# Layer 1's dense products cut into four of 32 outputs each, placed in the column groups of the PE array

## The chip, the core and the metric

The kernel runs on one core of a Trainium2 chip. A core has a tensor engine (PE, a 128 x 128 array that multiplies a stationary operand, loaded by its own weight-load instruction, with a moving operand, and writes to the PSUM memory), a vector engine (DVE), a scalar engine (ACT), a general engine (POOL) and queues for transfers. The metric is the device time of one execution in microseconds (us).

## What is computed

Two attention layers over x of shape (1, 128, 256, 256), that is 128 rows of 256 positions with 256 channels. Layer 0 is an attention with bias and gate. The change touches layer 1 alone:

```python
x = x + layer1(group_norm(x))            # layer1 for each of the 128 rows:
qkv = x2 @ w_in.T + b_in                 # 256 -> 3 * 256
q, k, v = split(qkv, 3)                  # four heads of 64
scores = q @ k.T / sqrt(64)              # only where |i - j| <= 16
out = softmax(scores) @ v
y = out @ w_out.T + b_out
```

All operands are float32.

## The kernel before

Layer 1 goes through the 128 rows in 64 pairs. The group norm's scale is folded into w_in once, its mean is taken off when a row is turned. `P` is 128, `C` 256, `I` 256, `KC` (chunks of channels) 2, `NB` (blocks of positions in a row) 2, `N2` 512 (positions of a pair), `H1` four heads, `DH` 32. `mm1` gives one of two PSUM banks of 512 columns. In each call of `matmul(out, stationary, moving)` the stationary operand's columns become the partitions of the output.

The parts of `Pair1` that the change touches:

```python
def turn(self, k):                       # channels onto partitions
    ...
    ps = mm1("ps_x1")
    for t in range(2 * NB):
        nc.tensor.transpose(ps[:, t * P : (t + 1) * P], self.xt[:, t, k * P : (k + 1) * P], ident)
    nc.scalar.activation(self.xgT[:, k, :], ps, AF.Identity, bias=nM1[:, k : k + 1])
    ...
def project(self, which, m):             # q and k, transposed
    ...
    for k in range(KC):
        nc.tensor.matmul(
            ps, w_in[:, k, n * C + m * P : n * C + (m + 1) * P], self.xgT[:, k, :],
            start=(k == 0), stop=(k == KC - 1),
        )
    nc.scalar.activation(...)            # ps to SBUF, with the bias
def values(self, r):
    ...
    for b in range(NB):
        t = r * NB + b
        for k in range(KC):
            nc.tensor.matmul(
                ps[:, b * C : (b + 1) * C], self.xgT[:, k, t * P : (t + 1) * P], w_in[:, k, 2 * C : 3 * C],
                start=(k == 0), stop=(k == KC - 1),
            )
    nc.scalar.copy(...)
def out_row(self, r):
    ...
    for b in range(NB):
        for k in range(KC):
            nc.tensor.matmul(
                ps[:, b * C : (b + 1) * C], self.oT[r][:, k, b * P : (b + 1) * P], w_out[:, k, :],
                start=(k == 0), stop=(k == KC - 1),
            )
    nc.vector.tensor_tensor(...)         # add the residual, to the output tile
```

Scores and apply use parts of the array already: scores 64 rows by 64 columns (a head's 64 channels, half of the 128 keys of a block), apply 64 rows by 32 columns. The schedule of one turn of the loop, written by hand:

```python
now.scores(0); was.apply(1); was.out_row(0); was.combine(1)
nxt.project("qT", 0); nxt.project("kT", 0); nxt.project("qT", 1)
nn.turn(0)

now.scores(1); now.apply(0); now.combine(0)
nxt.project("kT", 1); nxt.values(0); nxt.values(1)
was.out_row(1)
nn.turn(1)
```

Layer 0 has one product of the form that the change brings to layer 1, four heads side by side with 32 outputs each, which the prediction refers to:

```python
for b in range(NB):
    for q in range(HQ):                  # HQ = 4, D0 = 32
        h = c * HQ + q
        nc.tensor.matmul(
            ov[q * D0 : (q + 1) * D0, :], self.v[:, r, b, h * D0 : (h + 1) * D0],
            es[q // 2][:, q % 2, b, :], start=(b == 0), stop=(b == NB - 1),
        )
for q in range(HQ):
    nc.tensor.matmul(su[q * D0 : (q + 1) * D0, :], ...)   # sums of the weights, the same way
```

Of the kernel before, what the change touches and what calls it, by code (L numbers as in the profile page):

```python
# [16 lines left out]
P = 128  # L17
# [4 lines left out]
def bcast(ap, axis, n):  # L22

    ap = ap.unsqueeze(axis)
    shape = list(ap.shape)
    shape[axis] = n
    return ap.broadcast_to(shape)
# [746 lines left out]
def fast_kernel(  # L774
# [25 lines left out]
    nc = tc.nc  # L800
    S, I, C = x.shape
# [3 lines left out]
    H1, D1, BAND = 4, 64, 16  # L805
# [3 lines left out]
    KC = C // P  # L809
# [9 lines left out]
    ident = const.tile([P, P], F32, name="ident")  # L819
# [14 lines left out]
    def load_chunks(src, n, name):  # L834
        t = const.tile([P, src.shape[0] // P, n], F32, name=name)
        queued.append((t, src.rearrange("(k p) n -> p k n", p=P)))
        return t
# [71 lines left out]
    def rows(ap, s0, n):  # L909
        return ap[s0 : s0 + n].rearrange("s (b p) c -> p (s b) c", p=P)  # L910
# [17 lines left out]
    w_in = load_chunks(w_inT, 3 * C, "w_in")  # L928

    w_out = const.tile([P, KC, C], F32, name="w_out")  # L930
    for a in range(KC):
        for h in range(H1):
            n = P // H1
# [5 lines left out]
    for h in range(H1):  # L939
        n = P // H1  # L940
# [270 lines left out]
    class Pair:  # L1211
# [48 lines left out]
        def turn(self, pss=None):  # L1260
            self.xgT = la.tile([P, KC, N2], F32, name="xgT", tag="xgT", bufs=2)
            if pss is None:
                ps = ps_s.tile([P, KC, N2], F32, name="ps_x", tag="s")
                pss = [ps[:, k, :] for k in range(KC)]
            for k in range(KC):
                for t in range(NT):
                    nc.tensor.transpose(
                        pss[k][:, t * P : (t + 1) * P], self.xg[:, t, k * P : (k + 1) * P], ident
                    )
            for k in range(KC):  # L1270
                nc.scalar.copy(self.xgT[:, k, :], pss[k])
# [6 lines left out]
        def project(self, which, m):  # L1278
            w, src, b, fn, sc = {
                "gT": (wg, "xgT", bg_c, AF.Tanh, 0.5),  # L1280
                "qT": (wq, "xnT", qb, AF.Identity, 1.0),
                "kT": (wk, "xnT", kb, AF.Identity, 1.0),
            }[which]
            if m == 0:
                pool, bufs = (lb, 1) if which == "gT" else (la, 2)
                setattr(self, which, pool.tile([P, KC, N2], F32, name=which, tag=which, bufs=bufs))
            ps = mm("ps_p")
            for k in range(KC):
                nc.tensor.matmul(  # L1289
                    ps, w[:, k, m * P : (m + 1) * P], getattr(self, src)[:, k, :],  # L1290
                    start=(k == 0), stop=(k == KC - 1),
                )
            nc.scalar.activation(  # L1293
                getattr(self, which)[:, m, :], ps, fn, bias=b[:, m : m + 1], scale=sc
            )

        def values(self, r):
            if r == 0:
                self.v = la.tile([P, 2, NB, C], F32, name="v", tag="v", bufs=2)
            self.ps_v = mm("ps_v")  # L1300
# [4 lines that stand above are left out]
                        self.ps_v[:, b * C : (b + 1) * C], self.xnT[:, k, t * P : (t + 1) * P], wv[:, k, :],  # L1305
                        start=(k == 0), stop=(k == KC - 1),
                    )
# [80 lines left out]
        def out_row(self, r):  # L1388
            nonlocal xo
            s = 2 * self.p + r  # L1390
            if s % GB == 0:
                xo = lb.tile([P, GB * NB, C], F32, name="xo", tag="xo", bufs=2)
            self.ps_y = mm("ps_y")
# [3 lines that stand above are left out]
                        self.ps_y[:, b * C : (b + 1) * C], self.oT[r][:, k, b * P : (b + 1) * P], wo[:, k, :],  # L1397
                        start=(k == 0), stop=(k == KC - 1),
                    )
# [106 lines left out]
    behind, nx, n = None, 0, 0  # L1506
# [41 lines left out]
    with tc.manual_schedule():  # L1548
        old = was = Nobody()
        es = nn3 = None  # L1550
        for p in range(NP):
# [3 lines left out]
            ps = now.scores(0, 0)  # L1555
# [15 lines left out]
            ps = now.scores(0, 1)  # L1571
# [13 lines left out]
            ps = now.scores(1, 0)  # L1585
# [12 lines left out]
            ps = now.scores(1, 1)  # L1598
# [49 lines left out]
    DH = P // H1  # L1648
    LATE = 8
    rsum1 = dram.tile([NP, H1, 2, I], F32, name="rsum1")  # L1650
    with tc.tile_pool(name="l1", bufs=2) as sb, tc.tile_pool(
# [5 lines left out]
        def mm1(name):  # L1657
            return ps_mm.tile([P, 512], F32, name=name, tag="mm")
# [4 lines left out]
        for k in range(KC):  # L1663
            ps = mm1("ps_mr")
# [9 lines left out]
        for n in range(2):  # L1674
            nc.vector.memset(o_eo[n], 0.0)
            nc.vector.memset(su_eo[n], 0.0)

        class Pair1:


# [7 lines left out]
            def turn(self, k):  # L1688
                if k == 0:
                    self.xgT = sb.tile([P, KC, N2], F32, name="xgT1", tag="xgT")  # L1690
                ps = mm1("ps_x1")
                for t in range(2 * NB):
                    nc.tensor.transpose(ps[:, t * P : (t + 1) * P], self.xt[:, t, k * P : (k + 1) * P], ident)  # L1693
                nc.scalar.activation(self.xgT[:, k, :], ps, AF.Identity, bias=nM1[:, k : k + 1])  # L1694
                if k == KC - 1:
                    nc.gpsimd.tensor_tensor(self.xt, self.xt, bcast(bout_r, 1, 2 * NB), ALU.add)  # L1696

            def project(self, which, m):
                n = ("qT", "kT").index(which)
                if m == 0:  # L1700
                    setattr(self, which, sb.tile([P, KC, N2], F32, name=f"{which}1", tag=which))
                ps = mm1("ps_p1")
                for k in range(KC):
                    nc.tensor.matmul(  # L1704
                        ps, w_in[:, k, n * C + m * P : n * C + (m + 1) * P], self.xgT[:, k, :],
                        start=(k == 0), stop=(k == KC - 1),
                    )
                nc.scalar.activation(
                    getattr(self, which)[:, m, :], ps, AF.Identity, bias=bin_c[:, n * KC + m : n * KC + m + 1]
                )  # L1710

            def values(self, r):
                if r == 0:
                    self.v = sb.tile([P, 2, NB, C], F32, name="v1", tag="v")
                ps = mm1("ps_v1")
                for b in range(NB):
                    t = r * NB + b
                    for k in range(KC):
                        nc.tensor.matmul(  # L1719
                            ps[:, b * C : (b + 1) * C], self.xgT[:, k, t * P : (t + 1) * P], w_in[:, k, 2 * C : 3 * C],  # L1720
                            start=(k == 0), stop=(k == KC - 1),
                        )
                nc.scalar.copy(self.v[:, r, :, :].rearrange("p b c -> p (b c)"), ps)

            def scores(self, r):
# [60 lines left out]
            def out_row(self, r):  # L1786
                if r == 0:
                    self.yo = sb.tile([P, 2 * NB, C], F32, name="yo", tag="yo")
                ps = mm1("ps_y1")
                for b in range(NB):  # L1790
                    for k in range(KC):
                        nc.tensor.matmul(  # L1792
                            ps[:, b * C : (b + 1) * C], self.oT[r][:, k, b * P : (b + 1) * P], w_out[:, k, :],
                            start=(k == 0), stop=(k == KC - 1),
                        )
                nc.vector.tensor_tensor(  # L1796
                    self.yo[:, r * NB : (r + 1) * NB, :], ps.rearrange("p (b c) -> p b c", b=NB),
                    self.xt[:, r * NB : (r + 1) * NB, :], ALU.add,
                )
                s0 = 2 * self.p  # L1800
                if self.p == NP - 1:
                    nc.sync.dma_start(rows(out, s0 + r, 1), self.yo[:, r * NB : (r + 1) * NB, :])
                elif r == 1:
                    nc.sync.dma_start(rows(out, s0, 2), self.yo)
# [81 lines left out]
        ps = mm1("ok_ps")  # L1886
# [4 lines left out]
@with_exitstack  # L1891
def mixer_kernel(ctx, tc, *args):

    nc = tc.nc
    keep = ctx.enter_context(tc.tile_pool(name="verdict", bufs=1))
    verdict = keep.tile([1, 1], mybir.dt.int32, name="verdict")
    fast_kernel(tc, *args, verdict)
    again = nc.values_load(verdict[0:1, 0:1], min_val=0, max_val=1)
    with tc.If(again > 0):
        general_kernel(tc, *args)  # L1900
# [53 lines left out]
```

## Time and profile before

| | |
|---|---|
| time, median of 3 runs | 3370.32 us (3369.57 to 3371.17) |
| profiled span | 3366.7 us |
| PE busy | 3221.6 us, 96% of the span |
| weight loads (PEld) busy | 2032.1 us, 60% |
| DVE busy | 2024.1 us, 60% |
| ACT busy | 1463.3 us, 43% |
| POOL busy | 1975.2 us, 59% |
| mean granted PE clock | 0.983 |

Layer 1's first product starts at about 2119 us, and the rest of the span belongs to it. In the profile's names L1693 is the transposes (tile `ps_x`), L1704 the projections (`ps_p`), L1719 the values (`ps_v`), L1792 the output (`ps_y`), L1733 the scores (`ps_sc`), L1761 apply (`ps_o`, and `ps_su` for its sums). A group's row gives line, engine, operation, output and inputs, for a product the rows * columns of the array that it uses, partitions x elements, the count, busy time, mean length of one, and the idle time before it. Products overlap and their ends are modelled, so what a stage costs is read from the start of its first product to the start of the next stage.

### The profile page before, as it was taken

What the parts mean: (1) busy time and instruction counts of PE and PEld (TensorE: products, weight loads), DVE (VectorE), ACT (ScalarE), POOL (GpSimd) and SP (SyncE); (2) the same over time, 40 slices, a digit from 0 to 9 for tenths busy, and PEclk for the clock granted to TensorE, in tenths of its full rate; (3) what the DMA queues carried; (4) which work ended last, traced back from release to release, by engine and by line L of the source; (5) the groups of instructions that cost most, each with busy time, mean ns of one, the idle gap of its engine ahead of it and who ended that gap; (6) DMA issues with size and microseconds to landing.
All of it is one profiled execution on the core that took longest, in us unless ns stands there. A gap on an engine that the chain in (4) does not pass through costs nothing. (4 is left out here: it accounts for less than half of the span.)

```text
span 3366.7 us, 81193 instructions
## 1 busy us (share of the span) xinstructions
PE 3221.6 (96%) x35158; PEld 2032.1 (60%) x35158; DVE 2024.1 (60%) x3218; ACT 1463.3 (43%) x2121; POOL 1975.2 (59%) x1377
## 2 busy tenths in 40 slices
PE   5389999999999999999999998899999999999998
PEld 3245555555555555555555554567767777677676
DVE  7966666666666666666666666366544444443456
ACT  2264444444444444444444443344444444444443
POOL 2378787777777787887777874333333333333332
PEclk8699999999999999999999999999999999999999
DMA  9951212221222222122212221211211211212111
GB/s 351 367 136 43 72 49 73 74 73 48 73 74 60 55 71 68 48 73 74 74 49 73 74 63 45 68 58 53 64 53 52 65 53 55 62 52 62 56 57 53
DMA packets 198831, 262.91 MB, mean 78 GB/s; under 512 B 46304, under 2 KB 147552, under 8 KB 197312
## 3 DMA queue, kind: packets, MB, share of 16 engines
q1 hardware_dynamic: 193392, 254.72, 24.8%
q8 instruction: 279, 4.57, 0.7%
q10 hardware_dynamic: 5072, 2.90, 0.3%
q14 instruction: 88, 0.72, 0.1%
HBM read 188.82 MB, written 68.75 MB: 77 GB/s over the span
## 5 line engine op out<-in xcount | busy, mean ns | idle before, releaser
L1344 POOL TENSOR_TENSOR eboth<-e 128x512 f32<-128x512 f32 x512 | 640.4, 1272 | 389.4 <-DVE e L1339 389.4
L1339 DVE TENSOR_TENSOR e<-ps_sc,eb 128x1024 f32<-128x1024 f32 x512 | 603.0, 1219 | 316.4 <-ACT ps_sc L1330 227.2
L1330 ACT ACTIVATE ps_sc<-ps_sc 128x1024 f32<-128x1024 f32 x512 | 492.8, 1006 | 507.4 <-PE ps_sc L1323 507.4
L1743 POOL TENSOR_TENSOR e<-e,bw 128x384 f32<-128x384 f32 x256 | 259.6, 1037 | 443.5 <-ACT e L1741 443.5
L1704 PE MATMUL ps_p<-xgT,w_in 128*128 128x512 f32 x1024 | 468.1, 600 | 0.1
L1696 POOL TENSOR_TENSOR xt<-xt,bout_r 128x1024 f32<-128x1024 f32 x64 | 152.0, 2376 | 378.4 <-PE ps_x L1693 375.1
L1796 DVE TENSOR_TENSOR yo<-ps_y,xt 128x512 f32<-128x512 f32 x128 | 88.4, 691 | 380.0 <-PE ps_y L1792 380.0
L1704 PEld LDWEIGHTS ps_p<-xgT,w_in 128*128 128x128 f32 x1024 | 188.5, 190 | 199.0 <-issue 165.6
L1323 PE MATMUL ps_sc<-qT,kT 32*128 32x256 f32 x4096 | 293.7, 400 | 2.1 <-ACT kT L1293 2.1
L1354 PE MATMUL ps_ov<-e,v 128*32 128x256 f32 x4096 | 274.1, 385 | 0.5 <-DVE oT L1368 0.5
L1289 PE MATMUL ps_p<-xnT,wq 128*128 128x512 f32 x512 | 254.1, 618 | 0.7 <-POOL xnT L1276 0.6
L1289 PE MATMUL ps_p<-xgT,wg 128*128 128x512 f32 x512 | 253.9, 618 | 0.0
L1792 PE MATMUL ps_y<-w_out,oT 128*128 128x256 f32 x1024 | 250.1, 387 | 2.6 <-DVE oT L1777 2.6
L1396 PE MATMUL ps_y<-wo,oT 128*128 128x256 f32 x1024 | 243.9, 381 | 7.1 <-POOL oT L1386 7.1
L1396 PEld LDWEIGHTS ps_y<-wo,oT 128*128 128x128 f32 x1024 | 195.7, 191 | 88.1 <-issue 59.7
L1323 PEld LDWEIGHTS ps_sc<-qT,kT 32*128 32x128 f32 x4096 | 185.4, 184 | 94.4 <-issue 70.5
L1304 PE MATMUL ps_v<-wv,xnT 128*128 128x256 f32 x1024 | 242.1, 379 | 0.0
L1289 PE MATMUL ps_p<-xnT,wk 128*128 128x512 f32 x512 | 240.6, 592 | 0.0
L1719 PE MATMUL ps_v<-w_in,xgT 128*128 128x256 f32 x1024 | 231.8, 379 | 0.0
L1774 DVE RECIPROCAL rv<-odd 128x256 f32<-128x256 f32 x128 | 224.4, 1753 | 4.4
L1719 PEld LDWEIGHTS ps_v<-w_in,xgT 128*128 128x128 f32 x1024 | 194.4, 190 | 53.5 <-issue 30.1
L1304 PEld LDWEIGHTS ps_v<-wv,xnT 128*128 128x128 f32 x1024 | 189.6, 190 | 50.9 <-issue 31.1
(163 smaller groups left out, 4978.1 us busy)
## 6 DMA issues: line engine op xcount, KB each, us to landing
xa<-in_x_dram SPq DMA_DIRECT2D x8, 4096.0 KB
xt<-in_x_dram SPq DMA_DIRECT2D x64, 512.0 KB
rvb<-rsum SPq DMA_DIRECT2D x256, 128.0 KB
x<-xo SPq DMA_DIRECT2D x16, 2048.0 KB
xt<-x SPq DMA_DIRECT2D x64, 512.0 KB
out_dram<-yo SPq DMA_DIRECT2D x63, 512.0 KB
zt<-in_z_dram SPq DMA_DIRECT2D x15, 2048.0 KB
rs_r<-rs_d SPq DMA_DIRECT2D x63, 256.0 KB
```

What stands on the lines that cost most here:

```text
L1289: nc.tensor.matmul(ps, w[:, k, m * P : (m + 1) * P], getattr(self, src)[:, k, :], start=(k == 0), stop=(k == KC - 1),)
L1304: nc.tensor.matmul(self.ps_v[:, b * C : (b + 1) * C], self.xnT[:, k, t * P : (t + 1) * P], wv[:, k, :], start=(k == 0), stop=(k == KC - 1),)
L1323: nc.tensor.matmul(self.pss[q // 2][:, q % 2, b, :], self.kT[rs, c, r * I + b * P : r * I + (b + 1) * P], self.qT[rs, c, r * I : (r + 1) * I],
L1330: nc.scalar.activation(self.pss[a], self.pss[a], AF.Exp)
L1339: nc.vector.tensor_tensor(e, pss[a], eb[:, h : h + 2], ALU.mult)
L1344: nc.gpsimd.tensor_tensor(t, es[a][:, :, 0, :], es[a][:, :, 1, :], ALU.add)
L1354: nc.tensor.matmul(ov[q * D0 : (q + 1) * D0, :], self.v[:, r, b, h * D0 : (h + 1) * D0], es[q // 2][:, q % 2, b, :], start=(b == 0), stop= ...
L1396: nc.tensor.matmul(self.ps_y[:, b * C : (b + 1) * C], self.oT[r][:, k, b * P : (b + 1) * P], wo[:, k, :], start=(k == 0), stop=(k == KC - 1),)
L1704: nc.tensor.matmul(ps, w_in[:, k, n * C + m * P : n * C + (m + 1) * P], self.xgT[:, k, :], start=(k == 0), stop=(k == KC - 1),)
L1719: nc.tensor.matmul(ps[:, b * C : (b + 1) * C], self.xgT[:, k, t * P : (t + 1) * P], w_in[:, k, 2 * C : 3 * C], start=(k == 0), stop=(k == ...
L1743: nc.gpsimd.tensor_tensor(e[:, q], e[:, q], bcast(bw.rearrange("p b w -> p (b w)"), 1, KC), ALU.mult)
L1792: nc.tensor.matmul(ps[:, b * C : (b + 1) * C], self.oT[r][:, k, b * P : (b + 1) * P], w_out[:, k, :], start=(k == 0), stop=(k == KC - 1),)
```

## The change

Every dense product of layer 1 is cut into four. Each takes 32 of the 128 columns of the stationary operand and writes 32 of the 128 partitions of the same PSUM bank, so that the four fall into different column groups of the array and may run side by side. The transposes become ordinary products with the identity as moving operand, cut the same way. The aim is that the dense products use the array in column groups, as scores and apply do, with short weight loads for each group. Scores, apply, the evacuations and the schedule stay.

```diff
--- before.py
+++ after.py
@@ -1675,6 +1675,11 @@
             nc.vector.memset(o_eo[n], 0.0)
             nc.vector.memset(su_eo[n], 0.0)
 
+
+
+        def quarters(m):
+            return [slice(m * P + q * DH, m * P + (q + 1) * DH) for q in range(H1)]
+
         class Pair1:
 
 
@@ -1690,7 +1695,8 @@
                     self.xgT = sb.tile([P, KC, N2], F32, name="xgT1", tag="xgT")
                 ps = mm1("ps_x1")
                 for t in range(2 * NB):
-                    nc.tensor.transpose(ps[:, t * P : (t + 1) * P], self.xt[:, t, k * P : (k + 1) * P], ident)
+                    for at, of in zip(quarters(0), quarters(k)):
+                        nc.tensor.matmul(ps[at, t * P : (t + 1) * P], self.xt[:, t, of], ident, start=True, stop=True)
                 nc.scalar.activation(self.xgT[:, k, :], ps, AF.Identity, bias=nM1[:, k : k + 1])
                 if k == KC - 1:
                     nc.gpsimd.tensor_tensor(self.xt, self.xt, bcast(bout_r, 1, 2 * NB), ALU.add)
@@ -1701,10 +1707,10 @@
                     setattr(self, which, sb.tile([P, KC, N2], F32, name=f"{which}1", tag=which))
                 ps = mm1("ps_p1")
                 for k in range(KC):
-                    nc.tensor.matmul(
-                        ps, w_in[:, k, n * C + m * P : n * C + (m + 1) * P], self.xgT[:, k, :],
-                        start=(k == 0), stop=(k == KC - 1),
-                    )
+                    for at, of in zip(quarters(0), quarters(n * KC + m)):
+                        nc.tensor.matmul(
+                            ps[at], w_in[:, k, of], self.xgT[:, k, :], start=(k == 0), stop=(k == KC - 1)
+                        )
                 nc.scalar.activation(
                     getattr(self, which)[:, m, :], ps, AF.Identity, bias=bin_c[:, n * KC + m : n * KC + m + 1]
                 )
@@ -1716,10 +1722,11 @@
                 for b in range(NB):
                     t = r * NB + b
                     for k in range(KC):
-                        nc.tensor.matmul(
-                            ps[:, b * C : (b + 1) * C], self.xgT[:, k, t * P : (t + 1) * P], w_in[:, k, 2 * C : 3 * C],
-                            start=(k == 0), stop=(k == KC - 1),
-                        )
+                        for at, of in zip(quarters(0), quarters(t)):
+                            nc.tensor.matmul(
+                                ps[at, b * C : (b + 1) * C], self.xgT[:, k, of], w_in[:, k, 2 * C : 3 * C],
+                                start=(k == 0), stop=(k == KC - 1),
+                            )
                 nc.scalar.copy(self.v[:, r, :, :].rearrange("p b c -> p (b c)"), ps)
 
             def scores(self, r):
@@ -1789,10 +1796,11 @@
                 ps = mm1("ps_y1")
                 for b in range(NB):
                     for k in range(KC):
-                        nc.tensor.matmul(
-                            ps[:, b * C : (b + 1) * C], self.oT[r][:, k, b * P : (b + 1) * P], w_out[:, k, :],
-                            start=(k == 0), stop=(k == KC - 1),
-                        )
+                        for at, of in zip(quarters(0), quarters(b)):
+                            nc.tensor.matmul(
+                                ps[at, b * C : (b + 1) * C], self.oT[r][:, k, of], w_out[:, k, :],
+                                start=(k == 0), stop=(k == KC - 1),
+                            )
                 nc.vector.tensor_tensor(
                     self.yo[:, r * NB : (r + 1) * NB, :], ps.rearrange("p (b c) -> p b c", b=NB),
                     self.xt[:, r * NB : (r + 1) * NB, :], ALU.add,
```

## The prediction, made before the changed kernel was run

> **What bounds the kernel now.** I read the page's slices and chain first, to learn whether the tensor engine (PE) sets the end in layer 1, then the timeline of PE for a few microseconds, to see what each stage costs from start to start, then the groups with shapes kept apart, to count instructions.
>
> The window table (columns: window, length, then busy time and count of PE, weight loads, DVE, ACT and POOL, granted clock, DMA share, GB/s) and the page's chain:
>
> ```profile
> 2400.00:2800.00 400.00, 400.00 (x6413) 282.66 (x6412) 171.77 (x212) 176.90 (x291) 129.17 (x104) 1.00 0.19 57
> ...
> PE 37%; DVE 0%; ACT 0%; issue 0%; ACTq 0%
> PE ps_p L1704 13%; PE ps_y L1792 7%; PE ps_v L1719 7%; PE ps_o L1761 3%; PE ps_sc L1733 3%; PE ps_x L1693 2%; PE ps_su L1761 1%; DVE rv L1774 0%; DVE oT L1777 0%; DVE yo L1796 0%; DVE odd L1775 0%; DVE odd L1773 0%; ACT xgT L1694 0%; PE ps_mr L1666 0%; DVE chk L959 0%
> ```
>
> In layer 1 PE is busy all 400 of 400 us at full clock, the next engine 177 us. The chain is PE alone. So layer 1 lasts as long as its PE stages take back to back; other engines matter only if the change delays PE through them.
>
> The timeline of PE in layer 1 (start, length, line, operation, rows*columns of the array used, shape, count). A length runs past the next start because products overlap; costs are read from **start to start**:
>
> ```profile
> 2610.75 0.60 PE L1761 MATMUL ps_su<-e,ones 64*32 64x96 f32 x30
> 2611.28 1.99 PE L1792 MATMUL ps_y<-w_out,oT 128*128 128x256 f32 x8
> 2613.11 5.31 PE L1704 MATMUL ps_p<-xgT,w_in 128*128 128x512 f32 x12
> 2618.26 0.60 PE L1693 MATMUL ps_x<-ident,xt 128*128 128x128 f32 x4
> 2618.79 0.89 PE L1733 MATMUL ps_sc<-qT,kT 64*64 64x96 f32 x32
> 2619.61 0.93 PE L1761 MATMUL ps_o<-e,v 64*32 64x96 f32 x60
> ...
> 2620.90 1.98 PE L1704 MATMUL ps_p<-xgT,w_in 128*128 128x512 f32 x4
> 2622.72 3.62 PE L1719 MATMUL ps_v<-w_in,xgT 128*128 128x256 f32 x16
> 2626.18 1.89 PE L1792 MATMUL ps_y<-w_out,oT 128*128 128x256 f32 x8
> 2627.90 0.60 PE L1693 MATMUL ps_x<-ident,xt 128*128 128x128 f32 x4
> 2628.43 0.89 PE L1733 MATMUL ps_sc<-qT,kT 64*64 64x96 f32 x32
> ```
>
> One pair of rows is 2611.28 to 2630.55 (the next y after su in the same listing), 19.27 us. Rates: p 5.15 us / 12 = 429 ns for 512 moving columns; v 3.46 / 16 = 216 ns for 256. Both are 0.84 ns a column, whatever the stage: the array streams without a hole, and the 190 ns weight loads lie wholly beneath it. Holes appear only where the form of the array changes. The first y after su takes 1.83 us against 1.72 for the same 8 that follow v: 0.11 us for a first weight load that nothing hides. The four transposes take 0.53 us to the first score: 4 x 0.11 us and some 0.09 us of draining.
>
> Counts, from the groups with shapes kept apart (last two figures before the idle time: busy us, mean ns of one):
>
> ```profile
> L1704 PE MATMUL ps_p<-xgT,w_in 128*128 128x512 f32 x1024 | 468.1, 600 | 0.1
> L1693 PE MATMUL ps_x<-ident,xt 128*128 128x128 f32 x512 | 77.6, 275 | 0.2 <-DVE R1c L1668 0.2
> ```
>
> The program has 64 pairs x 4 projections x 2 chunks = 512 projection products, and the trace has 1024: **an ordinary f32 product is two instructions**. It has 64 x 2 x 4 = 512 transposes, and the trace has 512: **a transpose is one**.
>
> [...]from the last score start (end of the x32 group, 82 ns a round) to the first ps_o start the hole beyond streaming is about 0.09 us, though both forms are tiled.[...]
>
> **Is a column-tiled product slower or faster by itself?** Layer 0 already runs this form, four heads side by side with 32 outputs each:
>
> ```profile
> 1204.85 1.07 PE L1354 MATMUL ps_ov<-e,v 128*32 128x256 f32 x16
> 1205.73 0.61 PE L1360 MATMUL ps_su<-eboth,pick 128*32 128x256 f32 x8
> 1206.28 1.98 PE L1289 MATMUL ps_p<-xgT,wg 128*128 128x512 f32 x4
> ```
>
> 16 instructions take 0.88 us from 1204.85 to 1205.73. [...]four abreast, and a round as long as one wide product of 256 columns (216 ns). So splitting a wide product in four costs nothing in the stream and gains nothing either: the array was full before.
>
> **The change, part by part.** Per pair:
>
> 1. Projections, values and output: 48 instructions become 192, four abreast, 48 rounds. By the layer 0 rows a round equals the old instruction: 16 x 429 + 32 x 216 ns = 13.8 us before and after. **0 us.**
> 2. Transposes: 8 instructions of 110 ns become 8 x 4 quarters x 2 = 64 instructions, 16 rounds of 128 moving columns. [...]16 x 109 = 1.74 us against 8 x 110 = 0.88 us: **+0.87 us**, all on the path, since PE sets the end. Over 64 pairs +55.5 us.
> 3. The first weight load after each apply (before y, and before p): [...]Two a pair: **-0.16 us**, -10 us in all.
> 4. The four quarters of a round start some 7 ns apart, so the last ends 20 ns later, which shows where scores must wait for the array to drain, twice a pair: **+0.04 us**, +2.5 us in all. The 7 ns are my reading of how closely starts of one round follow each other in ov.
> 5. Drains at changes of form: x to scores, scores to apply, apply to p or y, three in each half before, three after. **0 us.**
> 6. Evacuations: an ACT evacuation of a 512-column bank takes about 690 ns, and a bank takes 0.87 us (transposes, now) or 1.72 us to fill, with two banks. They stay hidden. The transposes' bank even gets longer to fill (0.44 us before).
>
> Sum: +0.87 - 0.16 + 0.04 = +0.75 us a pair, 19.27 to 20.02; x 64 = +48 us. 3370.3 + 48 = **3418 us**, 1.4% slower. Layer 0 is untouched.
>
> **Rivals.**
>
> *The drains go.* If the engine passes between 128*32 and 64*32 without a drain because the column groups are the same, four of six drains a pair fall away (apply to p or y, x to scores): 4 x 0.09 x 64 = 23 us, giving 3395. For it: column groups keep their place between these two forms. Against it: scores (64*64) to apply (64*32) keeps the row groups and still shows the hole[...]. I give it one chance in six.
>
> *The narrow products starve.* PE must be handed 512 weight-load-and-product pairs per pair of rows (48 x 4 + 64 + the 256 of scores and apply) where it was 312. In apply, su's 30 instructions go out in 0.53 us, 17.7 ns each, against 10 if eight 80 ns streams were always abreast, so some limit near 17 ns a pair exists. The new transposes need one each 27 ns and projections one each 107, so they stay under it; but transposes come closest. If a transposing pair took 35 ns, 64 x 8 ns x 64 = +33 us, giving about 3450. I give it one chance in six.
>
> *The four streams clash.* In ov each quarter streams another tile; here all four stream the same xgT, w_in or identity at nearly the same moment. If that cost 5% of the 13.8 us, +44 us, 3462; if they ran only two abreast, +880 us. Nothing in the trace shows a case of it; one chance in twelve.
>
> *A gain in the stream.* For it, wide products would need holes now; 429 and 216 ns are both 0.84 ns a column, so there are none. I see no way to 2% faster.
>
> **Range and chances.** 3418 with the drains' rival at the low end (3395) and the starving one at the high end (3450). The 2% line lies at 3437.7. Below 3302.9 only a mechanism I can't see would lead.
>
> **What would show it.** The trace after should have 4096 instructions each of p, v, y and x (1024, 1024, 1024, 512 before); ps_x from first start to first score about 0.98 us instead of 0.53 (step 2); p's four rounds still about 1.72 us and v's 16 rounds 3.45 (step 1); first y after su about 1.75 instead of 1.83 (step 3); the hole before scores and after su still near 0.09 us (step 5). A pair of rows should take 20.0 us. I am wrong if v or p rounds grow (clash), if ps_x takes much over 1 us (starving), if the holes close (drains), or if the transposes remain one instruction each.

## The result and the profile after

The changed kernel takes **3444.74 us** (3442.56 to 3446.32) against 3370.39 us in the same runs: a ratio of 1.022, 95% interval 1.0202 to 1.0238. It is 74 us slower, where the prediction had 48. The time lies in the stated range, near its upper end, but the forecast of 1.4% lies on one side of the 2% line and the 2.2% that came on the other.

From the page of the changed kernel: its span, its engines, its instruction queue (packets, MB, share) and the chain of work that ended last:

```profile
span 3444.5 us, 106793 instructions
PE 3288.2 (95%) x47958; PEld 1933.0 (56%) x47958; DVE 2013.7 (58%) x3218; ACT 1469.1 (43%) x2121; POOL 1972.8 (57%) x1377
...
q8 instruction: 378, 6.19, 0.8%
...
PE 38%; issue 0%; DVE 0%; ACT 0%
```

PE still sets the end alone. It has 47958 products instead of 35158, and one row is worth a look that the prediction left out: the queue that brings instructions to the core moved 378 packets, 6.19 MB. Before it was

```profile
q8 instruction: 279, 4.57, 0.7%
```

6.19 MB over 378 is 16 KB a packet. PE's two rows and its semaphore waits make 96,479 instructions, 255 for each packet. Before, 70,879 instructions over 279 packets gave 254. So this queue is taken to be PE's own, and **a packet to be a piece of 256 instructions**.

A regular pair of rows in the timeline of PE after (the columns are those of the prediction's timeline):

```profile
2624.32 1.93 PE L1800 MATMUL ps_y<-w_out,oT 128*32 128x256 f32 x32
2626.07 5.33 PE L1711 MATMUL ps_p<-xgT,w_in 128*32 128x512 f32 x48
2631.22 1.06 PE L1699 MATMUL ps_x<-ident,xt 128*32 128x128 f32 x32
2632.21 0.89 PE L1740 MATMUL ps_sc<-qT,kT 64*64 64x96 f32 x32
2633.03 0.93 PE L1768 MATMUL ps_o<-e,v 64*32 64x96 f32 x60
...
2634.32 1.92 PE L1711 MATMUL ps_p<-xgT,w_in 128*32 128x512 f32 x16
2636.06 3.64 PE L1726 MATMUL ps_v<-w_in,xgT 128*32 128x256 f32 x64
2639.51 1.91 PE L1800 MATMUL ps_y<-w_out,oT 128*32 128x256 f32 x32
2641.24 1.06 PE L1699 MATMUL ps_x<-ident,xt 128*32 128x128 f32 x32
2642.23 0.89 PE L1740 MATMUL ps_sc<-qT,kT 64*64 64x96 f32 x32
...
2644.34 0.85 PE L1800 MATMUL ps_y<-w_out,oT 128*32 128x256 f32 x12
```

From y to y it is 20.02 us, the sum of the prediction to the hundredth. Values take 3.45 us as before, the first y 1.75 instead of 1.83, the transposes 0.98 to 0.99 instead of 0.53. So 64 x 0.75 = 48 us are found where they were expected. The other 26 us are not in a regular pair at all. They are here:

```profile
2613.42 0.95 PE L1768 MATMUL ps_su<-e,ones 64*32 64x96 f32 x30
2614.30 1.92 PE L1711 MATMUL ps_p<-xgT,w_in 128*32 128x512 f32 x16
...
3378.82 1.92 PE L1800 MATMUL ps_y<-w_out,oT 128*32 128x256 f32 x28
3382.43 0.41 PE L1800 MATMUL ps_y<-w_out,oT 128*32 128x256 f32 x2 [1.70 <-issue]
3382.45 0.62 PE L1711 MATMUL ps_p<-xgT,w_in 128*32 128x512 f32 x2
```

In the first case 30 sums take 0.88 us to the next stage instead of the usual 0.53. In the second PE stands idle for 1.70 us in the middle of an output row, and no semaphore (the signal by which one engine waits for another) ended the idle time: "issue" is time in which the engine waited for nothing that the profile shows. The waits of the whole span have three such rows for PE, which the kernel before has none of (columns: us in total, times, longest):

```profile
PE ps_y L1800 <- issue: 4.0, 5, 1.7
PE ps_p L1711 <- issue: 2.8, 6, 0.8
PE ps_su L1768 <- issue: 1.6, 5, 0.4
```

These rows count only what sticks out beyond the modelled ends of products still running, so the real loss is larger. In the records of the change, 17 times more than 0.55 us pass between one start on PE and the next (2160 to 3405 us). Each time PE went on 1.25 to 1.56 us after a packet of the instruction queue had landed, and a packet itself takes 1.01 us (median). And each of the 17 breaks, whether it falls in y, p or su, stands behind the same place of the count: behind record 193 of a block, when PE's records are counted from the start of the program in blocks of 256. I take this place for the end of one piece and the start of the next.

### The profile page after: what moved, and what is told of

It is laid out like the page before. It is cut to its first block, busy times and chain, and to the rows that moved or that the text cites. A ratio compares the mean times of both kernels' runs of the same rounds, so it can differ in the third digit from the quotient of the medians.

```text
span 3444.5 us, 106793 instructions
## 1 busy us (share of the span) xinstructions
PE 3288.2 (95%) x47958; PEld 1933.0 (56%) x47958; DVE 2013.7 (58%) x3218; ACT 1469.1 (43%) x2121; POOL 1972.8 (57%) x1377
## 3 DMA queue, kind: packets, MB, share of 16 engines
q8 instruction: 378, 6.19, 0.8%
## 5 line engine op out<-in xcount | busy, mean ns | idle before, releaser
L1711 PE MATMUL ps_p<-xgT,w_in 128*32 128x512 f32 x4096 | 479.0, 594 | 2.9 <-issue 2.8
L1711 PEld LDWEIGHTS ps_p<-xgT,w_in 128*32 128x32 f32 x4096 | 142.9, 110 | 249.2 <-issue 199.1
L1800 PE MATMUL ps_y<-w_out,oT 128*32 128x256 f32 x4096 | 253.5, 381 | 6.7 <-issue 4.0
L1726 PE MATMUL ps_v<-w_in,xgT 128*32 128x256 f32 x4096 | 235.8, 379 | 0.0
L1780 DVE TENSOR_TENSOR odd<-ps_su,odd 128x256 f32<-128x256 f32 x128 | 53.6, 419 | 302.2 <-ACT odd L1778 302.2
```

The costliest lines, as they stand in the source:

```text
L1711: nc.tensor.matmul(ps[at], w_in[:, k, of], self.xgT[:, k, :], start=(k == 0), stop=(k == KC - 1))
L1726: nc.tensor.matmul(ps[at, b * C : (b + 1) * C], self.xgT[:, k, of], w_in[:, k, 2 * C : 3 * C], start=(k == 0), stop=(k == KC - 1),)
L1800: nc.tensor.matmul(ps[at, b * C : (b + 1) * C], self.oT[r][:, k, of], w_out[:, k, :], start=(k == 0), stop=(k == KC - 1),)
```

## The experiments

**The two theories.** F: the regular pair is as predicted, and the rest is PE running out of instructions. A packet of 256 takes about 1 us to arrive, and at a hole PE went on 1.25 to 1.56 us after that; how long before its start it was asked for, the trace doesn't show. Transposes, scores and apply, the quick run, are together 64 + 64 + 192 = 320 instructions in 3.1 us, some 100 a microsecond. In none of the kernels here do two of these packets start less than 3.2 us apart in layer 1, which is 80 instructions a microsecond at best. By this estimate the quick run uses up more than arrives for a while. S: the narrow products and transposes themselves cost more than was read, spread over the stages.

In each trace I read two things: the regular pair (the commonest time from one pair's first score to the next pair's) and what the other pairs have on top, called stalls below. For the change they add up to 24 us; the other 2 of the 26 lie in the first and last pairs.

**Halves instead of quarters.**

```diff
-            return [slice(m * P + q * DH, m * P + (q + 1) * DH) for q in range(H1)]
+            return [slice(m * P + q * 64, m * P + (q + 1) * 64) for q in range(2)]
```

> The change with halves of 64 columns in place of quarters of 32, so that a pair of rows takes 384 weight-load-and-product pairs instead of 512, with the same streaming. Theory F (PE runs out of instructions in bursts: the regular pair of rows costs 20.02 us, and the other 26 us of the 74 are stalls while a piece of 256 instructions is fetched): a regular pair of 20.05 us[...] and hardly any stall, near 3420 us. Theory S (the narrow products and the narrow transposes themselves cost more than 20.02 a pair): half or all of the excess stays, 3432 to 3445 us.

Measured: 3418.45 us, ratio 1.0144 (1.0127 to 1.0161). The regular pair is 20.05 us, the stalls 0.4 us in all 62 pairs. In the timeline, first y to first projection and transposes to scores:

```profile
2609.10 1.04 PE L1699 MATMUL ps_x<-ident,xt 128*64 128x128 f32 x16
2610.08 0.89 PE L1740 MATMUL ps_sc<-qT,kT 64*64 64x96 f32 x32
...
2612.19 1.95 PE L1800 MATMUL ps_y<-w_out,oT 128*64 128x256 f32 x16
2613.97 5.32 PE L1711 MATMUL ps_p<-xgT,w_in 128*64 128x512 f32 x24
```

0.98 us of transposes and 1.78 us of y, as in the quarters (0.98 to 0.99 and 1.75) but for 0.03 us of y, which I put down to a first load of 64 columns in place of 32. The same streaming with a quarter fewer weight-load-and-product pairs gives the 48 us without the 26. It is no luck of the place: a pair has 772 instructions here, four more than three pieces, so in 62 pairs the quick run stands at nearly every place within a piece. That speaks for F.

**More instructions, the same streaming.**

```diff
-                for k in range(KC):
-                    for at, of in zip(quarters(0), quarters(n * KC + m)):
-                        nc.tensor.matmul(ps[at], w_in[:, k, of], self.xgT[:, k, :], ...)
+                for h in range(2):
+                    hs = slice(h * I, (h + 1) * I)
+                    for k in range(KC):
+                        for at, of in zip(quarters(0), quarters(n * KC + m)):
+                            nc.tensor.matmul(ps[at, hs], w_in[:, k, of], self.xgT[:, k, hs], ...)
```

> The change with every projection quarter cut further into two products of 256 moving columns: the same streaming (32 rounds of 216 ns instead of 16 of 429, +0.05 us a pair or 3 us in all), but 576 weight-load-and-product pairs for a pair of rows instead of 512. Theory F: more pieces to fetch, so more stalls, 3455 to 3490 us. Theory S: 3448 us.

Measured: 3471.89 us, ratio 1.0301 (1.0284 to 1.0318). The shortest pairs, those without a stall, take 20.06 us, so 64 x 0.79 = 51 us are regular and the other 51 us stalls. PE's bare waits, 8.4 us in the change, are 24.1 us:

```profile
PE ps_p L1713 <- issue: 16.3, 22, 1.6
PE ps_y L1802 <- issue: 4.8, 6, 1.8
PE ps_su L1770 <- issue: 3.0, 10, 0.5
```

**The place within a piece.** In the trace of the change the stalls are not spread evenly: each of the 20 pairs between some 2210 and 2620 us has one, and none of the 12 between 2784 and 3024 us. A pair has 1028 instructions, four more than four pieces, so the quick run drifts slowly through the pieces. Two kernels stop the drift and differ only in where it stops:

```diff
+            pad = mm1("pad")                               # ahead of the loop
+            for n in range(36):                            # the second kernel: 56
+                nc.tensor.matmul(pad[:DH, n : n + 1], ident[:, :DH], ident[:, n : n + 1], start=True, stop=True)
...                                                          # in out_row
+                            last = r == 1 and b == 1 and q == 3
+                            if last and k == 1:
+                                continue
...
```

Both leave out one product of a pair: 32 positions of every other row lack half of their channels' sum.

> In the trace of the change a pair of rows has 1028 instructions on PE's two rows, 4 more than four pieces of 256, so that from pair to pair the scores' place within a piece drifts by 4, and stalls come and go with that place: none at places 32 to 63, 1.0 to 1.5 us a pair at places 112 to 127. This kernel leaves one of the 512 products of a pair out (the second channel chunk of the output's last quarter, so 32 positions of every other row lack half of their channels' sum; the other three quarters of the round still stream, so no streaming time goes), which makes it 1024, and puts 36 products of one column ahead of the loop, so that the place stays at about 39. Theory F: no stalls, 3370 + 48 + 2 = 3420 us. If the place means nothing: 3445 us.

> The same as the experiment with 36 products ahead of the loop, with 56 of them, so that the place of the scores within a piece of 256 instructions stays at about 119. Theory F: some 1.3 us of stalls in nearly every pair, 3370 + 48 + 3 + 80 = 3500 us. If the place means nothing: 3446 us.

Measured: **3418.86 us**, ratio 1.0145 (1.0128 to 1.0161), with 36, and **3496.43 us**, ratio 1.0376 (1.0359 to 1.0394), with 56. Twenty one-column products ahead of the loop cost 78 us, though the 56 take only 1.2 us longer than the 36 (3.5 and 2.3 us in the records). With 36 every pair is regular, 20.01 to 20.05 us. With 56 the stall sits in every pair at the same spot, after the first four projection products, which follow apply and the first output row:

```profile
2795.09 5.33 PE L1711 MATMUL ps_p<-xgT,w_in 128*32 128x512 f32 x48
2800.24 1.06 PE L1699 MATMUL ps_x<-ident,xt 128*32 128x128 f32 x32
```

is the good place, and this the bad one, with its row of the waits:

```profile
2817.23 1.03 PE L1711 MATMUL ps_p<-xgT,w_in 128*32 128x512 f32 x4
2818.73 4.92 PE L1711 MATMUL ps_p<-xgT,w_in 128*32 128x512 f32 x42 [0.47 <-issue]
...
PE ps_p L1711 <- issue: 12.1, 42, 0.5
```

Of the four products two start at 2817.23 and two at 2817.66, so not even the first round of four was complete; the next began 1.50 us after the first. In this kernel 41 breaks of over 0.55 us are on record, and again each stands behind record 193 of a block of 256 (so do all 31 of the kernel with more instructions). The piece that ends there runs in 3.45 us. In the kernel with halves 13 pieces run in under 2.5 us and have no hole behind them, so the time of one piece alone doesn't tell. No theory in which the narrow products themselves cost more can tell these two kernels apart. S falls.

**Where the quick run stands.** The transposes moved ahead of the projections (first half) and ahead of the values (second half):

```diff
                 was.combine(1)
+                nn.turn(0)
                 nxt.project("qT", 0)
                 ...
-                nn.turn(0)
```

> The change, all instructions the same and as many, with the transposes moved ahead of the projections (first half) and ahead of the values (second half), so that the quick run of transposes, scores and apply (320 instructions in 3.1 us) is cut to scores and apply (256 in 2.1 us) behind slow projections and outputs. Theory F: the regular pair stays 20.0 us and the stalls shrink, 3419 to 3430 us. Theory S: nothing changes, 3445 us.

Measured: 3671.98 us, ratio 1.09 (1.0881 to 1.0918). The experiment missed its aim, for it moved the transposes five microseconds closer to the load of their rows:

```profile
2604.64 1.93 PE L1800 MATMUL ps_y<-w_out,oT 128*32 128x256 f32 x32
2610.09 1.08 PE L1699 MATMUL ps_x<-ident,xt 128*32 128x128 f32 x32 [3.52 <-DVE odd L1782]
...
2633.86 1.08 PE L1699 MATMUL ps_x<-ident,xt 128*32 128x128 f32 x32 [3.40 <-DMA xt<-x]
```

In one pair the wait of some 3.5 us is put down to a vector instruction and in the next to the load. It is the load in both, for with the load a pair earlier it goes:

```diff
-                self.xt = sb.tile([P, 2 * NB, C], F32, name="xt1", tag="xt", bufs=4)
+                self.xt = sb.tile([P, 2 * NB, C], F32, name="xt1", tag="xt", bufs=5)
...
-                nn = pair1(p + 2)
+                nn2 = pair1(p + 3)
```

> The change with the transposes moved ahead of the projections and of the values as in the experiment before, and the load of a pair's rows issued one pair earlier into a fifth buffer, so that the transposes no longer wait for it. The regular pair should be near 20.2 us (0.1 us of waiting for a PSUM bank in the second half), 3370 + 58 = 3428 us. Theory F: instructions as many as in the change, but the quick run is 256 long instead of 320, so fewer stalls: 3428 to 3442 us. Theory S, or stalls that follow from the number of instructions alone: 3452 us or more.

Measured: 3448.78 us, ratio 1.0231 (1.0214 to 1.0248). The time alone would count against F, but the regular pair is 20.37 us and not 20.2, since the projections in the first half wait for a PSUM bank too (transposes to projections 1.05 us instead of 0.87; their loads wait for the vector instruction that empties the output's bank 56 times, up to 0.6 us, and in the change 45 times, up to 0.4). That is 64 x 1.10 = 70 us of the 79; the stalls in its trace add up to 5 us where the change has 24, with as many instructions. So the mechanism holds, and my estimate of the new order's own cost was wrong.

**The transposes and the changes of form.** Three kernels with one part each.

```diff
-                    nc.tensor.transpose(ps[:, t * P : (t + 1) * P], self.xt[:, t, k * P : (k + 1) * P], ident)
+                    nc.tensor.matmul(ps[:, t * P : (t + 1) * P], self.xt[:, t, k * P : (k + 1) * P], ident, start=True, stop=True)
```

> The kernel before with one change: each transpose is an ordinary product with the identity, in one piece of 128 outputs, so that no column group is used. If the lost transpose mode is the cost (step 2): 8 more instructions of 110 ns a pair, +0.88 us a pair, +56 us, 3426 us, and no stalls. If the cost comes from the cutting in four: 3370 us.

Measured: 3426.49 us, ratio 1.0171 (1.0154 to 1.0188). The regular pair is 20.17 us, +0.91, without stalls. The group and the stage:

```profile
L1693 PE MATMUL ps_x<-ident,xt 128*128 128x128 f32 x1024 | 136.4, 277 | 0.1
...
2622.75 1.05 PE L1693 MATMUL ps_x<-ident,xt 128*128 128x128 f32 x8
2623.74 0.89 PE L1733 MATMUL ps_sc<-qT,kT 64*64 64x96 f32 x32
```

Twice the instructions, 0.99 us to the scores, and not one product cut. The cost of the transposes lies in the ordinary products (before, 512 instructions and 0.53 us to the scores) and not in the column groups.

The transposes alone cut in quarters, all else as before:

> The kernel before with the transposes alone cut in quarters. By the steps: +0.87 us for the second pass, and a new change of form ahead of the transposes[...]: a pair of 20.41 us, +73 us, 3443 us. If changes of form between whole and column-tiled products cost nothing: 3426 us. Stalls, with 736 instructions a pair: few (theory F).

Measured: 3452.53 us, ratio 1.0244 (1.0226 to 1.0261). The regular pair is 20.42 us against 20.41 expected. The change of form ahead of the transposes shows in y, 1.82 us where it took 1.73:

```profile
2602.06 1.89 PE L1796 MATMUL ps_y<-w_out,oT 128*128 128x256 f32 x8
2603.88 1.08 PE L1697 MATMUL ps_x<-ident,xt 128*32 128x128 f32 x32
```

The 9 us beyond the 3443 expected are stalls, in 17 of 62 pairs, though this kernel has fewer instructions than the one with halves (307 packets against 314): it keeps the quick run of 320. So both the number and the length of the run count.

All but the transposes cut in quarters:

> The change without its part on the transposes: projections, values and output in quarters, transposes as before. By the steps of the prediction a pair is 19.27 - 0.16 (short first loads) [...]= 19.54 us, +17 us, 3388 us; with theory F up to 10 us of stalls on top (912 instructions a pair). The rival, that a change of form between column-tiled and whole products costs nothing: 3360 us.

Measured: 3386.76 us, ratio 1.0049 (1.0032 to 1.0065). The regular pair is 19.45 us, not 19.54:

```profile
2614.87 1.91 PE L1799 MATMUL ps_y<-w_out,oT 128*32 128x256 f32 x32
2616.71 0.66 PE L1698 MATMUL ps_x<-ident,xt 128*128 128x128 f32 x4
2617.30 0.89 PE L1739 MATMUL ps_sc<-qT,kT 64*64 64x96 f32 x32
```

The hole ahead of the transposes is there (1.84 instead of 1.73), but the four transposes take 0.585 us in the records instead of 0.53: I put the 0.055 us down to their bare load. It is half of what a first load of 128 columns adds to y behind apply (0.104 us in the trace of before: 0.320 us from the first start to the next, where others take 0.216), and I had put in the whole. With 64 x 0.18 = 11.5 us regular, some 5 us are stalls, in 10 pairs.

No experiment points to a version that beats the kernel before. The one gain of the change is 0.16 us a pair from shorter first loads, and the least that comes with it is a change of form ahead of whole transposes, 0.11 us and 0.055 twice a pair.

## Why the prediction was right, and where it was not

- **Step 1, the stream** (0 us): right. Values take 3.45 us before and after; four column groups carry what the whole array carried. Layer 0 shows it in the trace of before: its rounds of four start 0.215 to 0.216 us apart, behind a first one of 0.240, and wide products of 256 columns 0.215 to 0.216. The rival of clashing streams falls with it.
- **Step 2, the transposes** (+0.87 us a pair): right, and shown by the whole identity products, +0.91 us without any cutting. The 109 ns of a round was an estimate; rounds of the transposes start 0.109 to 0.110 us apart in the change. That a cut transpose has to be an ordinary product was not shown: no run here cuts one in its own form.
- **Step 3, the first load** (-0.16): right, 1.75 for 1.83 us ahead of the projections. Behind apply the first y starts 0.320 us ahead of the next before and its first round 0.240 us ahead in the change, where others take 0.216: 0.104 us bare and 0.024.
- **Step 4, the last quarter** (+0.04): an estimate, right within reading: transposes to scores 0.987 us in quarters as against 0.973 in halves.
- **Step 5, the drains**: right. They stay (scores to apply 0.82 us before and after), and the two kernels with a part cut show the further ones (y ahead of the transposes 1.82 and 1.84 us where it took 1.73). So the rival of vanishing drains falls.
- **Step 6, evacuations**: right for the change, whose chain has ACT and DVE at 0%; they came onto the path only where the order was altered (1.05 us for 0.87).
- **The sum** gave 20.02 us a pair, and a regular pair takes 20.02. What failed is that the sum had no term for the supply of instructions. The starving rival named this side and 3450 us, but as a steady rate that slows the transposes to 35 ns each. They take 27, that is (0.987 us less 0.11 of drain and last quarter) / 32. PE starves in single holes, up to 2.08 us from one start to the next, all behind record 193 of a block of 256. That missing term was 26 us, and it carried the time over the 2% line.
- **Luck**: the six steps explain 48 of the 74 us. That the whole still fell within 3395 to 3450 is luck of the place: with the 56 products ahead of the loop, and the same sum of steps, the time was 3496 us, outside the range.

## What to carry to other kernels

Cutting full products into column groups gained nothing in the stream here, where the whole products already streamed without a hole (the values take 3.45 us either way), and the transposes, made ordinary products, took twice the instructions (1024 for 512, uncut) and 0.99 us to the scores for 0.53. Look at how many instructions PE gets through in a run of small products: in this case 320 in 3.1 us gave holes marked "issue", and PE went on 1.25 to 1.56 us after a packet of the instruction queue had landed; there, twenty small products more ahead of the loop moved the time by 2.3% (3418.86 to 3496.43 us). How long a run must be for that was not measured: 288 in 3.1 us (the halves) gave next to none (0.4 us). A time that rests on such a place says little about a neighbouring variant; compare regular stretches of the timeline as well.

## What was not expected of the hardware

- Two kernels that differ by twenty one-column products ahead of the loop differ by 78 us (3418.86 and 3496.43), through the place of the loop's quick run within pieces of 256 instructions.
- After a hole, products start out of program order: at 3382.43 two outputs, at 3382.45 two projections, which stand behind those outputs in the program, then at 3382.65 outputs again.
- Behind apply, the first y took 0.10 us longer with 128 columns (1.83 against 1.73 in the middle of all pairs), 0.05 with 64 (1.78) and 0.02 with 32 (1.75), which I put down to a first weight load that nothing hides. Behind y in quarters, four transposes of 128 columns took only 0.055 us more (0.585 against 0.53).
